# A macaron block on one core: recurrences by channel half, replicated operands copied through DRAM, FFN scales moved from weights to activations

## The chip, the cores and the metric

The kernel runs on one core of one Trainium2 chip. The metric is the device time of one execution in microseconds; the figure quoted is the median of the runs. Engines are named as in the profile: PE is TensorE (matmuls), PEld its weight loads, DVE is VectorE, ACT is ScalarE, POOL is GpSimd, SP is the engine that issues every DMA of this kernel. Each engine runs its own instructions in a fixed order, which the compiler of the kernel language lays down in advance.

## The reference, cut to what matters

The input is 4 sequences of 512 tokens, 128 wide. Six residual stages follow each other; all arithmetic is fp32.

```python
x = x + 0.5 * ffn(layernorm(x))        # 128 -> 512 -> 512 -> 512 -> 128
x = x + mamba(layernorm(x))            # selective state-space layer
x = x + 0.5 * ffn(layernorm(x))        # same weights
x = x + 0.5 * moe(layernorm(x))        # 64 experts, top 8
x = x + attention(layernorm(x))        # 8 heads
x = x + 0.5 * moe(layernorm(x))        # same weights
```

The two parts that the change concerns:

```python
# ffn: a linear layer is (x @ w.T) * s, s one scale per output channel
h = silu(lin(x, w1, s1)) * lin(x, w2, s2)
h = gelu(lin(h, h1, sh1)); h = gelu(lin(h, h2, sh2))
return lin(h, w3, s3)

# mamba: 256 channels d, 16 states n, 512 times t
x_ssm, z = split(x @ in_proj.T)
xc = silu(conv4(x_ssm) + conv_b)
dt_r, B, C = split(xc @ x_proj.T)                       # 1, 16, 16
dt = softplus(dt_r * dt_w + dt_b)
h[t,d,n] = exp(dt[t,d]*A[d,n]) * h[t-1,d,n] + dt[t,d]*B[t,n]*xc[t,d]
y[t,d] = sum_n h[t,d,n]*C[t,n] + xc[t,d]*D[d]
return (y * silu(z)) @ out_proj.T
```

## The kernel before

Everything is held transposed: channels on the 128 partitions, the 512 tokens of one sequence along the free dimension. A sequence is called a batch `b`, 0 to 3. All weights fit in SBUF. A matmul of 128x128 weights with 512 columns appears as two records in the trace[...].

**First half** (`first_half`, L401 on). For each batch: FFN, mamba, FFN again. `ffn` (L219) and `mamba_rest` (L362) are generators; `first_half` interleaves them by hand. While the 16 steps of one batch's recurrence run on DVE and ACT, the `filler` feeds PE with steps of the FFNs of later or earlier batches, as many per step as the table `FILL` says (23 in batch 0, 12 in each of the others). `mamba_first` of the next batch is advanced one generator step at every second recurrence step from step 4 on. `early()` gives instructions a higher priority in the compiler's ordering; the order that comes out is fixed per engine.

**The recurrence.** 256 channels x 16 states = 4096 scans of length 512; one DVE scan instruction does 128 of them. A scan tile holds 32 channels (group `k`, 4 groups in each channel half `c`) by 4 states: partition `32*m + r` is channel `32*k + r` with state `4*m + q`. For this layout the operands must be replicated:

- `rep` (L354, `mamba_spread`): 32 rows of `both` (dt and dt*x, both channel halves, 8 KB a row) are copied from SBUF to SBUF four times, to partitions 0-31, 32-63, 64-95 and 96-127. One DMA per copy, 256 KB each, 16 a batch.
- `B`, `C` (L316-325): written to DRAM (`kept`, L315) and read back in eight DMAs, each with four rows repeated over 32 partitions, 256 KB each.

A step (q, k) then is: two ACT exponentials (`da`, L372, one per channel half), one DVE multiply by B (L374, 128x1024), two DVE scans (L376, 128x512 each), one DVE multiply by C (L377, 128x1024) and two matmuls with the 128x32 matrix `sum4` (L382) that add the four states of a tile into the PSUM accumulators `ys[0]` and `ys[1]`, one for each channel half. After 16 steps PE adds the skip term D*xc (L390), DVE multiplies by silu(z) (L394), PE applies `out_w` (L397) and DVE adds to `xs[b]` (L398). The second channel half is kept with its two 64-row halves exchanged (`HALF`: the split loads of `in_w` and `out_w`, and `skip`), and the copies of `rep` for groups 0 and 1 of the next batch are issued only after step 15.

**FFN scales.** Before the first layernorm the kernel multiplies the scales into the weights (L130-142): a diagonal matrix on DVE, a matmul with ones to spread it over the partitions, a DVE multiply of the weights. From then on activations act on 128x1024 tiles at once: silu (L248), product (L249), gelu (L261).

**PSUM.** `ps_acc` has two rotating banks under one tag, used by the recurrence, the MoE sums and attention; `ps_aux` has two; `pair` has two tiles of two banks.

**Second half** (`second_half`). MoE and attention, PE close to saturated. Its weights are loaded into the SBUF space of the mamba pool once that is free.

Of the kernel before, what the change touches and what calls it, by code (L numbers as in the profile page):

```python
# [29 lines left out]
P = 128  # L30
# [12 lines left out]
HALF = P // 2  # L43
EARLY = 3000
FILL = ((2, 1) * 7 + (1, 1), *[(0, 1, 1, 1) * 4] * 3)
# [11 lines left out]
def macaron(ctx: ExitStack, tc: tile.TileContext, a: dict, out: bass.AP):  # L57
# [7 lines left out]
    ps_acc = ctx.enter_context(tc.tile_pool(name="ps_acc", bufs=2, space=PSUM))  # L65
# [6 lines left out]
    def acc():  # L72
        return ps_acc.tile([P, S], F32, tag="acc", name="acc")
# [14 lines left out]
    nc.sync.dma_start(out=xs[0], in_=a["xT"][:, 0:S])  # L88
    vec = load("vec", [P, NV])
    w1 = load("w1", [P, HID], layer1)  # L90
    w2 = load("w2", [P, HID], layer1)
    h1 = load("h1", [P, NH, HID], layer1)
    h2 = load("h2", [P, NH, HID], layer1)
    w3 = load("w3", [P, NH, D], layer1)

    in_w = layer1.tile([P, 2 * DI], F32, tag="in_w", name="in_w")
    last = 2 * DI - P
    nc.sync.dma_start(out=in_w[:, 0:last], in_=a["in_w"][:, 0:last])
    for i in range(2):
        to, lo = last + i * HALF, last + (1 - i) * HALF  # L100
        nc.sync.dma_start(out=in_w[:, to : to + HALF], in_=a["in_w"][:, lo : lo + HALF])
    xp_w = load("xp_w", [P, NC, 1 + 2 * NST], layer1)
    dt_w = load("dt_w", [1, DI], layer1)
    out_w = layer1.tile([P, NC, D], F32, tag="out_w", name="out_w")
    nc.sync.dma_start(out=out_w[:, 0, :], in_=a["out_w"][:, 0, :])
    for i in range(2):
        to, lo = i * HALF, (1 - i) * HALF
        nc.sync.dma_start(out=out_w[to : to + HALF, 1, :], in_=a["out_w"][lo : lo + HALF, 1, :])
    neg_a = layer1.tile([P, NR, NC, NQ], F32, tag="neg_a", name="neg_a")
    for k in range(NR):  # L110
        for m in range(NM):
            for c in range(NC):
                lo = V_AL + c * NST + m * NQ
                nc.sync.dma_start(
                    out=neg_a[m * R : (m + 1) * R, k, c, :], in_=a["vec"][k * R : (k + 1) * R, lo : lo + NQ]
                )
    for b in range(1, NB):
        nc.sync.dma_start(out=xs[b], in_=a["xT"][:, b * S : (b + 1) * S])
# [9 lines left out]
    ones = layer1.tile([P, P], F32, tag="ones", name="ones")  # L128
    nc.gpsimd.memset(ones, 1.0)
    for w, v, n in ((w1, V_S1, NH), (w2, V_S2, NH), (h1, V_H1, NH), (h2, V_H2, NH), (w3, V_S3, 1)):  # L130
        ps = aux()[:, 0 : n * P]
        for c in range(n):
            d = ln.tile([P, P], F32, tag="diag", name="diag")
            if w is w3:
                nc.vector.tensor_scalar(d, ident, vec[:, v : v + 1], 0.5, ALU.mult, ALU.mult)
            else:
                nc.vector.tensor_scalar_mul(d, ident, vec[:, v + c : v + c + 1])
            nc.tensor.matmul(ps[:, c * P : (c + 1) * P], lhsT=ones, rhs=d, start=True, stop=True)
        if w is w1 or w is w2:
            nc.vector.tensor_mul(w, w, ps)  # L140
        else:
            nc.vector.tensor_mul(w, w, ps.unsqueeze(1).to_broadcast([P, NH, n * P]))
    nc.scalar.activation(neg_a, neg_a, AF.Exp)
    nc.vector.tensor_scalar_mul(neg_a, neg_a, -1.0)

    sum4 = layer1.tile([P, R], F32, tag="sum4", name="sum4")
    nc.vector.tensor_reduce(sum4, ident.rearrange("p (m r) -> p r m", m=NM), AX.X, ALU.add)
    skip = layer1.tile([P, NC, P], F32, tag="skip", name="skip")
    for c in range(NC):
        for i in range(2):  # L150
            to, lo = i * HALF, (i ^ c) * HALF
            nc.vector.tensor_scalar_mul(
                skip[:, c, to : to + HALF], ident[:, lo : lo + HALF], vec[:, V_DD + c : V_DD + c + 1]
            )
# [64 lines left out]
    def ffn(pool, pair, b):  # L219
# [21 lines left out]
        for c in range(NH // 2):  # L241
            p1, p2 = two(), two()
            for ps, w in ((p1, w1), (p2, w2)):
                for i in range(2):
                    product(ps, i, w, xn, c, 1)
            g = pool.tile([P, 2, S], F32, tag="g", name="g", bufs=1)
            with early():
                nc.scalar.activation(g, p1, AF.Silu)  # L248
                nc.vector.tensor_mul(h[:, 2 * c : 2 * c + 2, :], p2, g)  # L249
            yield  # L250
        for w in (h1, h2):
            nxt = pool.tile([P, NH, S], F32, tag="h", name="hn")
            both = [two(), two()]
            for c in range(NH // 2):
# [3 lines left out]
                if c:  # L258
                    with early():
                        for i in range(2):  # L260
                            act = nc.scalar.activation(nxt[:, 2 * i : 2 * i + 2, :], both[i], AF.Gelu)  # L261
                            if not i:
# [6 lines left out]
        with early():  # L269
            nc.vector.tensor_add(xs[b], ps, xs[b])  # L270
        yield

# [3 lines left out]
    def mamba_first(pool, b, made):  # L276
# [15 lines left out]
        with early():  # L292
            for c in range(NC):
                nc.vector.tensor_scalar_mul(cv[:, c, :], xi[:, c, 0:S], col(V_CW + c * DCONV))
                for k in range(1, DCONV):
                    nc.vector.scalar_tensor_tensor(
                        cv[:, c, :], xi[:, c, k : k + S], col(V_CW + c * DCONV + k), cv[:, c, :], ALU.mult, ALU.add
                    )
            for c in range(NC):
# [3 lines left out]
            for c in range(NC):  # L303
                nc.scalar.activation(xc[:, c, :], cv[:, c, :], AF.Silu, bias=col(V_CB + c))
# [8 lines left out]

        kept = dram.tile([2 * NST, S], F32, tag="kept", name="kept")
        nc.sync.dma_start(out=kept, in_=rows[1:])  # L315
        bcs = []  # L316
        for i, name in enumerate(("B", "C")):
            t = pool.tile([P, NQ, S], F32, tag="bcs", name=name, bufs=4)
            for m in range(NM):
                lo = NST * i + NQ * m  # L320
                nc.sync.dma_start(
# [528 lines left out]
```

## Time and profile before

| quantity | value |
|---|---|
| median of 3 runs | 1836.29 us (1835.99 to 1836.46) |
| the profiled execution | 1834.04 us, its span 1832.2 us |
| PE busy | 1717.3 us (94%) |
| DVE busy | 1123.2 us (61%) |
| ACT busy | 785.3 us (43%) |
| POOL busy | 4.3 us |
| DMA moved | 42.27 MB |
| chain that ended last | PE 72%, DVE 17%, ACT 7%, issue 3% |
| recurrence, DVE scans L376 | 128 x 1211 ns = 150.7 us (4.7 us idle before them) |
| recurrence, multiplies L374 and L377 | 64 x 1209 ns and 64 x 1216 ns |
| recurrence, exponentials L372 | 128 x 713 ns |
| gelu L261, silu L248 (128x1024) | 32 x 1021 ns, 16 x 1023 ns |
| table loads on ACT | 1283 ns each |

The span is one execution from its first to its last instruction; 1.8 us of the execution's time lie around it. "Busy" counts an engine's own instructions. PE's busy time is modelled from pipelined matmuls, so a busy PE can still be slower than its best. The chain of waits follows back from the last instruction what each one waited for.

### The profile page before, as it was taken

To read this page: it belongs to the slowest core of one execution; us is meant where nothing else is said; L and a number is where in the kernel's file an instruction comes from. 1 tells how busy PE (TensorE), PEld (TensorE's weight loads), DVE (VectorE), ACT (ScalarE), POOL (GpSimd) and SP (SyncE) were. 2 spreads that over 40 slices of the span, in tenths; PEclk is the share of its full clock that TensorE was granted. 3 is DMA by queue.
4 is the path that set the end of the run, shared out by engine and by line. 5 is a ranking of instruction groups with operands and counts; after the bars stand their busy time and mean duration, and the time that the engine had idled before them with its cause. 6 is when DMAs were issued, how large, how long until landed. Compare 5 with 4: busy or idle time off the path is not lost.

```text
span 1832.2 us, 13288 instructions
## 1 busy us (share of the span) xinstructions
PE 1717.3 (94%) x4466; PEld 749.4 (41%) x4466; DVE 1123.2 (61%) x1976; ACT 785.3 (43%) x1189; POOL 4.3 (0%) x22
## 2 busy tenths in 40 slices
PE   6999899785869999999999999999999999999999
PEld 3333232221224444444455445544554455444443
DVE  3127989798963656556566646665566466565554
ACT  3357647572543223223545345534454444422222
POOL 0000000000000000000000000000000000000000
PEclk9999999997989999999999999999999999999999
DMA  3062224242033000000000000000000000000000
GB/s 96 1 140 48 48 44 93 46 93 46 1 118 112 1 1 0 1 0 1 0 1 1 0 0 1 1 0 0 1 1 6 0 1 1 6 0 1 6 0 6
DMA packets 14441, 42.27 MB, mean 23 GB/s; under 512 B 5068, under 2 KB 6053, under 8 KB 11045
## 3 DMA queue, kind: packets, MB, share of 16 engines
q1 hardware_dynamic: 14373, 41.43, 9.1%
q8 instruction: 35, 0.57, 0.1%
q14 instruction: 33, 0.27, 0.0%
HBM read 23.33 MB, written 1.31 MB: 13 GB/s over the span
## 4 chain that ended last, share of the span: by engine, by line
PE 72%; DVE 17%; ACT 7%; issue 3%; DMA 0%; SPq 0%; DVEq 0%; ACTq 0%
PE acc L559 16%; PE pair L565 16%; PE pair L564 16%; DVE hs L376 7%; PE pair L225 6%; PE aux L620 4%; PE acc L658 4%; DVE hs L374 3%; DVE hs L377 2%; PE aux L648 2%; PE aux L605 2%; PE aux L612 2%; PE aux L196 1%; PE aux L190 1%; PE pair L268 1%
## 5 line engine op out<-in xcount | busy, mean ns | idle before, releaser
L567 ACT ACTIVATE g<-pair 128x512 f32<-128x512 f32 (+1 forms) x368 | 219.6, 597 | 645.6 <-PE pair L565 642.3
L570 DVE TENSOR_TENSOR gr<-g,rw 128x512 f32<-128x512 f32 x352 | 242.7, 691 | 342.0 <-ACT g L567 342.0
L559 PE MATMUL acc<-h,wd 128*128 128x512 f32 x704 | 362.5, 596 | 9.7 <-DVE h L573 9.6
L564 PE MATMUL pair<-xn,wg 128*128 128x512 f32 x704 | 359.9, 593 | 0.0
L565 PE MATMUL pair<-xn,wu 128*128 128x512 f32 x704 | 359.5, 592 | 0.0
L573 DVE TENSOR_TENSOR h<-gr,pair 128x512 f32<-128x512 f32 x352 | 240.4, 686 | 25.3 <-DVE gr L570 0.5
L559 PEld LDWEIGHTS acc<-h,wd 128*128 128x128 f32 x704 | 128.9, 189 | 176.6 <-DVE h L573 112.3
L565 PEld LDWEIGHTS pair<-xn,wu 128*128 128x128 f32 x704 | 133.4, 190 | 161.4 <-issue 158.8
L564 PEld LDWEIGHTS pair<-xn,wg 128*128 128x128 f32 x704 | 126.4, 190 | 120.4 <-issue 117.6
L376 DVE TENSOR_TENSOR_SCAN hs<-da,hs 128x512 f32<-128x512 f32 x128 | 150.7, 1211 | 4.7 <-ACT da L372 4.5
L382 PE MATMUL acc<-hs,sum 128*32 128x512 f32 x256 | 75.6, 672 | 53.3 <-DVE hs L377 52.9
L225 PE MATMUL pair<-h,h 128*128 128x512 f32 x256 | 119.8, 605 | 2.0 <-ACT g L248 1.9
L225 PE MATMUL pair<-hn,h 128*128 128x512 f32 x256 | 116.5, 601 | 4.2 <-ACT hn L261 4.2
L372 ACT ACTIVATE da<-rep,neg_a 128x512 f32<-128x512 f32 x128 | 84.9, 713 | 63.9 <-DVE hs L376 63.7
L620 PE MATMUL aux<-kt,q 128*128 128x512 f32 (+3 forms) x256 | 91.4, 441 | 4.1 <-ACT pt L653 2.7
L633 ACT ACTIVATE p<-p,a_low 128x128 f32<-128x128 f32 (+3 forms) x128 | 70.3, 550 | 31.5 <-DVE a_low L622 31.5
L374 DVE TENSOR_TENSOR hs<-rep,B 128x1024 f32<-128x1024 f32 x64 | 76.8, 1209 | 2.1 <-PE acc L382 2.1
L377 DVE TENSOR_TENSOR hs<-hs,C 128x1024 f32<-128x1024 f32 x64 | 77.8, 1216 | 0.3
L225 PEld LDWEIGHTS pair<-hn,h 128*128 128x128 f32 x256 | 46.7, 190 | 73.6 <-issue 60.9
L225 PEld LDWEIGHTS pair<-h,h 128*128 128x128 f32 x256 | 46.2, 190 | 74.6 <-issue 65.7
L658 PE MATMUL acc<-pt,vo 128*128 128x512 f32 (+3 forms) x256 | 76.2, 433 | 0.0
L225 PE MATMUL pair<-xn,w 128*128 128x512 f32 x128 | 65.1, 646 | 10.9 <-DVE xn L202 7.1
(145 smaller groups left out, 1454.1 us busy)
## 6 DMA issues: line engine op xcount, KB each, us to landing
rep<-both SPq DMA_DIRECT2D x64, 256.0 KB, 5.0
B<-kept SPq DMA_DIRECT2D x16, 256.0 KB, 4.6
C<-kept SPq DMA_DIRECT2D x16, 256.0 KB, 7.6
h<-in_h SPq DMA_DIRECT2D x2, 1024.0 KB, 8.4
wg<-in_wg SPq DMA_DIRECT2D x4, 384.0 KB, 7.3
wu<-in_wu SPq DMA_DIRECT2D x4, 384.0 KB, 7.4
wd<-in_wd SPq DMA_DIRECT2D x4, 384.0 KB, 7.4
wg<-in_wg SPq DMA_DIRECT2D x4, 320.0 KB, 7.2
```

What stands on the lines that cost most here:

```text
L225: m = nc.tensor.matmul(ps[:, i, :], lhsT=w[:, cut] if n == 1 else w[:, k, cut], rhs=h if n == 1 else h[:, k, :], start=k == 0, stop=k == n ...
L374: nc.vector.tensor_mul(h, t[:, 1], bs[:, q].unsqueeze(1).to_broadcast([P, NC, S]))
L376: nc.vector.tensor_tensor_scan(h[:, c, :], da[:, c, :], h[:, c, :], 0.0, ALU.mult, ALU.add)
L377: nc.vector.tensor_mul(h, h, cs[:, q].unsqueeze(1).to_broadcast([P, NC, S]))
L559: nc.tensor.matmul(po, lhsT=w, rhs=h, start=n == 0, stop=n == len(jobs) - 1)
L564: nc.tensor.matmul(pg, lhsT=wg_, rhs=xn, start=True, stop=True)
L565: nc.tensor.matmul(pu, lhsT=wu_, rhs=xn, start=True, stop=True)
L567: nc.scalar.activation(g, pg, AF.Silu)
L570: nc.vector.tensor_mul(gr, g, rw)
L573: nc.vector.tensor_mul(h, g, pu)
L620: nc.tensor.matmul(sc, lhsT=q[:, i * P : n], rhs=kt[:, 0:n], start=True, stop=True)
L658: nc.tensor.matmul(po[:, j * P :], lhsT=vo[:, j, h, :], rhs=pt[:, lo : lo + n], start=h == 0 and j == 0, stop=h == HEADS - 1 and j == NT - ...
```

## The change

**Recurrence.** The loop order becomes channel half `c`, pair of groups, state `q`. A step works on one channel half and two groups (`KP = 2` pairs), so tiles stay 128x1024 for the multiplies and 128x512 for scans and exponentials. Exponentials are asked for in blocks of four (two states, two groups) with high priority. There is one PSUM accumulator `ys`, begun with the skip matmul; the product with silu(z) follows each channel half, in place.

**Copies.** `both` is laid out by channel half and written to a DRAM tile `spread`, one DMA a half. `channels` reads two groups of 32 rows from there, each repeated four times, into a 16 KB-per-partition ring of two tiles. `states` reads one q of B and C at a time into a ring of five tiles. A group's successor is requested at the group's first step, and the next batch's in the last group. `mamba_first` of the next batch advances from step 0. For batch 0 the softplus is cut in two halves.

**FFN.** Weights stay unscaled. silu and gelu take the scale as a per-partition operand and work on 128x512; the product with the second branch becomes a scalar_tensor_tensor with its scale; the output is scaled by `half_s3` in the residual add.

**Loads and set-up.** The exchange of halves goes; `w1` comes before `vec`, `xs[1]` before `h1`; `h1` and `h2` are split in two; `neg_a` takes 8 DMAs instead of 32; what is left of the set-up (`prepare`) is put after four steps of the first FFN. `ps_acc` gets two tags of one bank, `ys` (recurrence, attention) and `po` (MoE).

```diff
-    for w, v, n in ((w1, V_S1, NH), (w2, V_S2, NH), (h1, V_H1, NH), (h2, V_H2, NH), (w3, V_S3, 1)):
-        ps = aux()[:, 0 : n * P]
-        for c in range(n):
-            d = ln.tile([P, P], F32, tag="diag", name="diag")
...
-            nc.tensor.matmul(ps[:, c * P : (c + 1) * P], lhsT=ones, rhs=d, start=True, stop=True)
...
-                nc.scalar.activation(g, p1, AF.Silu)
-                nc.vector.tensor_mul(h[:, 2 * c : 2 * c + 2, :], p2, g)
+                for i in range(2):
+                    f = 2 * c + i
+                    nc.scalar.activation(g[:, i, :], p1[:, i, :], AF.Silu, scale=col(V_S1 + f))
+                    nc.vector.scalar_tensor_tensor(
+                        h[:, f, :], p2[:, i, :], col(V_S2 + f), g[:, i, :], ALU.mult, ALU.mult
+                    )
...
+    def states(pool, b, made, q):
+        kept, _, bcs, _ = made[b][2:]
+        t = pool.tile([P, 2, S], F32, tag="bc", name="bc", bufs=5)
+        by_q = kept.rearrange("(i m q) t -> q m i t", i=2, m=NM)[q]
+        for i in range(2):
+            nc.sync.dma_start(
+                out=t[:, i, :], in_=by_q[:, i].unsqueeze(1).to_broadcast([NM, R, S])
+            )
+        bcs[q] = t
+
+    def channels(pool, b, made, c, pair):
+        _, spread, _, reps = made[b][2:]
+        t = pool.tile([P, 2, 2, S], F32, tag="rep", name="rep", bufs=2)
+        by_k = spread[c].rearrange("(k r) j t -> k r (j t)", k=NR)
+        for i in range(2):
+            nc.sync.dma_start(
+                out=t[:, i].rearrange("p j t -> p (j t)"),
+                in_=by_k[2 * pair + i].unsqueeze(0).to_broadcast([NM, R, 2 * S]),
+            )
+        reps[c, pair] = t
...
                 for step in range(4 * NQ):
+                    group, q = divmod(step, NQ)
+                    if q == 0:
+                        if group < 3:
+                            channels(pool, b, made, *divmod(group + 1, KP))
+                        elif more:
+                            channels(pool, b + 1, made, 0, 0)
+                            states(pool, b + 1, made, 0)
+                    elif group == 3 and more:
+                        states(pool, b + 1, made, q)
                     go(rest)
-                    if step >= 4 and step % 2 == 0:
+                    if step % 2 == 0:
                         go(nxt)
                     filler(FILL[b][step])
```

## The prediction

> **What bounds the kernel now.** I read the page's slices first, then the busy times of each recurrence, then the timeline of the start, then the DMA issues. The slices:
>
> ```profile
> span 1832.2 us, 13288 instructions
> PE   6999899785869999999999999999999999999999
> DVE  3127989798963656556566646665566466565554
> DMA  3062224242033000000000000000000000000000
> ```
>
> From slice 13 on (about 595 us) PE is full and the change touches nothing but bank tags there. All that can move lies before it: a start in which PE is not full, and slices 4 to 11, where DVE is. The busy times in windows cut at the last multiply by C of each batch (columns: window, length, then busy us and count of PE, PEld, DVE, ACT, POOL, granted clock, DMA share, GB/s):
>
> ```profile
> 142.30:241.30 99.00, 90.01 (x223) 30.11 (x221) 90.64 (x87) 60.25 (x73) 0.00 (x0) 0.98 0.31 65
> 241.30:334.00 92.70, 80.05 (x197) 25.95 (x196) 86.03 (x84) 60.71 (x74) 0.11 (x1) 0.98 0.31 65
> 334.00:437.50 103.50, 78.67 (x184) 24.18 (x184) 89.87 (x89) 60.34 (x74) 0.11 (x1) 0.88 0.30 61
> 437.50:525.90 88.40, 67.55 (x165) 21.43 (x166) 78.63 (x73) 39.12 (x48) 0.00 (x0) 0.92 0.03 5
> ```
>
> DVE is idle 8.4, 6.7, 13.6 and 9.8 us in the four batches: little to gain. Batch 0 is held by PE and DVE together. A step of undisturbed recurrence takes 4.5 us. The start and the copies in the timeline (start, us, engine, line):
>
> ```profile
> 0.73 0.38 SPq L88 DMA_DIRECT2D x<-in_xT  x1
> 19.20 2.07 PE L190 MATMUL aux<-x,mean_w 128*128 128x512 f32 x2 [1.95 <-DVE h L142]
> 28.23 7.41 PE L225 MATMUL pair<-xn,w 128*128 128x512 f32 x10 [3.45 <-DVE xn L202]
> 99.44 1.72 SPq L321 DMA_DIRECT2D B<-kept  x4
> 109.95 18.82 SPq L359 DMA_DIRECT2D rep<-both  x16
> 142.32 2.33 DVE L376 TENSOR_TENSOR_SCAN hs<-da,hs 128x512 f32<-128x512 f32 x2
> ```
>
> The first layernorm waits for the scaling of the weights (DVE h L142), not for x. What the DMA engines give, in a stretch of copies to 32 partitions and in one of weight loads to 128 (same columns), and two landing times from the page's issues:
>
> ```profile
> 111.00:128.00 17.00, 15.89 (x38) 6.76 (x37) 0.69 (x1) 5.63 (x6) 0.00 (x0) 1.00 1.00 206
> 540.00:560.00 20.00, 18.41 (x47) 8.13 (x48) 12.42 (x42) 11.31 (x12) 0.31 (x1) 1.00 1.04 393
> ...
> rep<-both SPq DMA_DIRECT2D x64, 256.0 KB, 5.0
> ...
> x<-in_xT SPq DMA_DIRECT2D x4, 256.0 KB, 3.1
> ```
>
> With all 16 engines busy a copy to 32 partitions moves 206/16 = 12.9 GB/s an engine, a load to 128 partitions 393/(16 x 1.04) = 23.6.
>
> [...] The old copies have 32 rows on both sides: 16 engines, and the share of 1.00 agrees. The new `channels` and `states` read with a leading dimension of NM = 4: four engines[...]. No run here shows that yet. [...] the trace has 597 ns for silu without (L567) and 685 to 721 with a bias (L337, L338, L304). I use 690.
>
> **Part 1, the start.** Gone: the 34 diagonal matmul records (10.3 us of PE) and their DVE work. The first layernorm then waits for x, which lands at 0.73 + 3.1 = 3.8 us, and not 19.2. From there to the first FFN matmul it takes the 28.23 - 19.20 = 9.0 us it took: 12.9 against 28.2, so -15.3 us. The matmul needs w1, second in the queue; the silu needs vec, third: both within about 3 us of x. h1 and h2 (2 MB) are wanted some 12 us later, and the old start moved 277 GB/s, so they are in by then. `prepare` is five small DVE operations and a 32-column exponential that lie beside the first FFN's matmuls. 24 fewer DMA issues of `neg_a` (14.96 us for 32 on SP) free that queue, on which nothing waits then. All that follows moves along: `kept` has landed by 99.44 - 15.3 = 84.1 us.
>
> **Part 2, FFN in halves.** ACT: 64 gelus x 690 - 31.0 us = +13, 32 silus x 690 - 16.4 = +5.7, over eight FFNs, 2.4 us each. ACT was busy 61 of 99 us in its fullest batch, which covers it; uncovered it would be 19 us. Against it a layer's first matmul waits for one tile, not two: I give neither a price. DVE: the scalar_tensor_tensor takes 746 ns (L296), so 2 x 746 - 1222 = +0.27 us for each of 16 pairs, +0.5 a batch.
>
> **Part 3, recurrence without its copies.** Per batch still 32 scans of 1.21 us and 32 multiplies of the same, 128 exponentials in all: no DVE work saved. Gone are the skip matmuls in front of the last product (DVE waited 2.9 to 4.0 us for them at the ends) and the wait for `rep` after step 15. Come: two products per batch that wait for the last `sum4` on PE, about 2 us each, and one accumulator bank, so the skip matmul of the next half stands in PE's queue until DVE has done the product; the filler matmuls behind it wait too, but PE has 13 to 25 us free in batches 1 to 3. So each batch is its DVE time + 0.5 + 6 us of waits: 97, 92.5, 96.4 and 85.1 against 99.0, 92.7, 103.5 and 88.4, in all -12.6. After the last step the 2.5 us of skip matmuls are gone: -2.5. The earlier `mamba_first` moves its 16 us of DVE work within the batch only. `po` on one bank: the MoE's first down matmul stands behind four gate and up matmuls of 0.86 us each, which hide the last add of the batch before; nothing, at worst 1 us in each of seven.
>
> **Part 4, the copies.** Four engines[...]. A `channels` request is 64 rows of 4 KB per engine, a `states` request 64 rows of 2 KB. Alone[...] an engine needs 174 and 87 ns a row (23.6 GB/s): 11.1 and 5.6 us a request. [...] In step all the way they get 12.9 GB/s: 318 and 159 ns, 20.3 and 10.2 us. Nothing shows how far they keep step; I take the middle, 15.7 and 7.9, and keep both ends.
>
> Batch 0 begins with four `states` requests, ready at 84.1 before the channels are; `spread` is written (landing 2.4 us: 3.1 less the 0.7 of the bytes, from x) behind them[...]; then `channels` and its landing. First scan: 84.1 + 4 x 7.9 + 2.4 + 15.7 + 2.4 = 136.2, against 142.3: -6.1, so the start's gain is half lost. (Ends: 122.4 and 150.0.) PE's queue still has FFN steps then.
>
> At each of three borders, the last group of a batch asks for one `channels` and four `states`, and the next batch's first group for another `channels`, which stands behind them. In the eight steps, 44 us, of those two groups the four engines owe 2 x 15.7 + 4 x 7.9 + 2.4 = 65.4: 21.4 late. While DVE waits it does the next batch's other work, of which some 6 us are caught up later: +15. (Ends: 47.0, +3; 83.8, +40 with nothing to catch up, for a group then needs 20.3 + 2.4 of its 22 us.) Inside a batch 15.7 + 2.4 fits in 22. ACT's exponentials, high in priority, stand first in its queue while they wait, with gelus behind them and PE behind those; PE's free time covers that. On SP a `channels` request that waits for its buffer would hold back `states`, `kept` and `spread` behind it; the buffer is that of two groups ago, free when it is asked for, so it waits for about nothing (before, L359 waited 62 us for L374 in this place, hidden).
>
> **Sum.** -6.1 - 12.6 - 2.5 + 3 x 15 = +24 us on the profiled execution's 1834.0: 1858. The median before is 2.3 us higher: 1860.
>
> **Rivals.** *The copies keep up* (0.27): the rows run at 174 ns[...]. -19.9 - 12.6 - 2.5 + 9 = -26: 1810. For it: 6.3 MB a batch are then 67 of some 92 us. Against: equal rows, equal order, one start. This is the case on the other side; between it and mine the sign turns at a row about 1.2 times as long as alone. *In step throughout* (0.22): +7.7 - 12.6 - 2.5 + 120 = +113: 1949; the copies alone take 4 x 122 us. *The copy is spread over 16 engines after all* (0.09), so that the change lacks the confinement I read into it: 2.8 and 1.4 us a request, no border wait; PE's own work then holds batch 0 to about 217 us, and -24 - 10 - 2.5 = -37: 1799. *A compiler order that loses the start's gain* (0.04): ACT or PE blocked for 15 to 20 us behind early exponentials: 1836 to 1842.
>
> **How the numbers follow.** Mine has 0.38 with its own range of 1830 to 1900, as the row goes from 1.2 to 1.6 times. Faster by over 0.2% (3.7 us, about what a measurement here tells from no change): 0.27 + 0.09 + 0.03 = 0.39; within it 0.05; slower 0.56. The range, 1797 to 1930, leaves out the upper part of the in-step case.
>
> **What would show it.** First FFN matmul at 13 us; else part 1 is wrong. DMA share about 0.25 with 50 to 100 GB/s while copies run: four engines; a share near 1: sixteen. DVE waiting for `rep` or `bc` by DMA, or for `da`, in the first eight steps of batches 1 to 3 is my case; no such wait refutes it. Landing of a first 512 KB `rep` copy (32 rows and 2.4 us): 8 us alone, 10 in my case, 12.6 in step. The recurrence should end near 549 us, not 526; 500 means that the copies kept up.

## The result, and the profile after

The changed kernel takes 1840.8 us, the kernel before 1834.7 us in runs beside it: the ratio is 1.0032, with a 95% interval of 1.0021 to 1.0042. It is slower by 6 us; 24 were forecast. The profiled execution took 1843.7 us, its span 1841.8.

The page's slices and its chain of waits, after:

```profile
span 1841.8 us, 13185 instructions
PE   8848978787899999999999999999999999999998
DVE  1238889798843655556466656664666466565554
DMA  3021212222041000000000000000000000000000
...
PE 69%; DVE 16%; DMA 7%; ACT 5%; issue 3%; SPq 0%; DVEq 0%; ACTq 0%
```

DMA has come into the chain with 7%; before it had none. In the third slice (92 to 138 us), PE has fallen from 9 tenths to 4. From about 595 us on PE is full again, as forecast. Who waits for the copies is in the answer on waits between 80 and 560 us (engine, line, what it waited for; us, times, longest; lines left out are marked):

```profile
ACT da L367 <- DMA rep<-spread: 92.9, 16, 19.0
...
PE ys L380 <- DVE hs L376: 55.6, 25, 25.5
DVE hs L373 <- DMA rep<-spread: 42.1, 2, 29.0
...
ACT L367 <- DMA rep<-spread: 37.6, 4, 21.9
...
PE pair L251 <- ACT hn L242: 23.6, 6, 11.7
...
DVE x L253 <- PE pair L251: 16.4, 5, 5.7
...
DVE hs L373 <- issue: 9.5, 1, 9.5
...
DVE h L228 <- ACT g L227: 7.9, 3, 4.2
...
DVE h L228 <- PE pair L202: 3.0, 2, 2.8
```

All of these go back to `rep`, by two ways. By the first, ACT stands before exponentials whose `rep` hasn't landed (130.5 us with the table loads that wait in the same place). The gelus (L242) are behind them in ACT's fixed order, PE's next FFN layer (L251) waits for the gelus, and DVE waits for both, with the residual add (L253) and the FFN's product (L228). By the second, DVE waits for `rep` itself (the 9.5 us without a releaser too, as the view of the copies' line, L347, shows), and PE, which has the sums of the recurrence (L380) in its own fixed order, waits for DVE. This is PE's largest wait.

The largest wait is in batch 0. From the timeline, SP's, ACT's and PE's instructions around it (start, us, engine, line; in brackets the idle time before and what ended it):

```profile
84.86 13.47 SPq L336 DMA_DIRECT2D bc<-kept  x8
98.45 3.12 SPq L326 DMA_DIRECT2D spread<-both  x2
110.94 56.02 SPq L347 DMA_DIRECT2D rep<-spread  x8
...
99.28 1.28 ACT L367 ACT_TABLE_LOAD   x1
119.57 0.72 ACT L367 ACTIVATE da<-rep,neg_a 128x512 f32<-128x512 f32 x1 [19.00 <-DMA rep<-spread]
124.64 4.40 ACT L367 ACTIVATE da<-rep,neg_a 128x512 f32<-128x512 f32 x7 [4.36 <-DMA rep<-spread]
129.73 0.72 ACT L367 ACTIVATE da<-rep,neg_a 128x512 f32<-128x512 f32 x1 [0.69 <-DMA rep<-spread]
134.81 4.40 ACT L367 ACTIVATE da<-rep,neg_a 128x512 f32<-128x512 f32 x7 [4.36 <-DMA rep<-spread]
...
98.16 7.99 PE L202 MATMUL pair<-hn,h 128*128 128x512 f32 x18 [0.50 <-ACT hn L242]
131.64 1.92 PE L380 MATMUL ys<-hs,sum 128*32 128x512 f32 x4 [25.48 <-DVE hs L376]
133.49 5.06 PE L202 MATMUL pair<-hn,h 128*128 128x512 f32 x6
138.48 1.05 PE L380 MATMUL ys<-hs,sum 128*32 128x512 f32 x4
```

`spread` is asked for at 98.45 and has landed at 110.94, behind eight requests for states. The two DMAs of the first channels request land at 119.57 and 124.64, those of the next at 129.73 and 134.81: 5.07 us from one DMA to its neighbour. Each is 128 rows of 4 KB; on four engines, as the share below shows, that is 32 rows an engine, 5.07/32 = 158 ns a row. PE does nothing for 25.5 us: it stands before the first sums of the recurrence. Two queues are blocked here. On PE, 18 of the 32 matmul records of an FFN layer (`pair<-hn,h`) have run, and the other 14 stand behind the sums, although the gelus that they read had ended at 99.26; at the 14.00 us that all 32 take elsewhere (run 7) they are about 6 us of work, an estimate. What follows that layer needs gelus, and these stand on ACT behind 17 exponentials; the table load at 99.28 with nothing behind it but waiting is the mark of that blocked queue. In the kernel before, all 32 records and FFN work after them stood ahead of the first sums:

```profile
110.63 14.00 PE L225 MATMUL pair<-hn,h 128*128 128x512 f32 x32 [2.68 <-ACT hn L261]
125.75 3.70 PE L268 MATMUL pair<-hn,w 128*128 128x512 f32 x8 [1.11 <-ACT hn L261]
...
145.97 1.05 PE L382 MATMUL acc<-hs,sum 128*32 128x512 f32 x4
```

How many engines run is in the windows (columns as in the prediction: window, length, busy us and count of PE, PEld, DVE, ACT, POOL, granted clock, DMA share, GB/s), here while nothing but a channels copy goes on:

```profile
114.00:124.00 10.00, 0.00 (x0) 0.00 (x0) 0.00 (x0) 0.72 (x1) 0.00 (x0) 0.50 0.26 97
```

A quarter of 16 engines, at 97/4 = 24 GB/s each. PE and DVE have no instruction in these 10 us.

Where the time went, by three marks: the first scan starts at 127.0 us (before 142.3), the last scan at 521.7 (523.4), and from there to the end of the span it takes 1320.1 us (1308.8). So the scans take 394.7 us from first to last against 381.1, and the remainder has grown by 11.3: in PE's order 132 matmul records of the FFNs come after the last scan, where the kernel before has 88. The three differences add up to the 9.6 us between the two spans; the medians lie 6.1 apart, since the profiled execution was the slowest of the changed kernel's eight.

### The profile page after: what moved, and what is told of

It reads as the page before. It is cut to its first block, busy times and chain, and to the rows that moved or that the text cites. A ratio compares the mean times of both kernels' runs of the same rounds, so it can differ in the third digit from the quotient of the medians.

```text
span 1841.8 us, 13185 instructions
## 1 busy us (share of the span) xinstructions
PE 1713.1 (93%) x4432; PEld 748.3 (41%) x4432; DVE 1114.6 (61%) x1974; ACT 801.1 (43%) x1243; POOL 4.2 (0%) x21
## 4 chain that ended last, share of the span: by engine, by line
PE 69%; DVE 16%; DMA 7%; ACT 5%; issue 3%; SPq 0%; DVEq 0%; ACTq 0%
PE po L561 16%; PE pair L566 15%; PE pair L567 15%; PE pair L202 6%; DVE hs L375 5%; DMA rep<-spread 5%; PE aux L622 4%; PE ys L660 4%; DVE hs L373 3%; DVE hs L376 2%; PE aux L650 2%; PE aux L607 2%; PE aux L614 2%; DMA spread<-both 1%; PE pair L251 1%
## 5 line engine op out<-in xcount | busy, mean ns | idle before, releaser
L561 PE MATMUL po<-h,wd 128*128 128x512 f32 x704 | 362.5, 596 | 10.8 <-DVE h L575 10.7
L561 PEld LDWEIGHTS po<-h,wd 128*128 128x128 f32 x704 | 128.7, 189 | 178.5 <-DVE h L575 114.0
L566 PEld LDWEIGHTS pair<-xn,wg 128*128 128x128 f32 x704 | 126.4, 190 | 120.4 <-issue 117.7
L380 PE MATMUL ys<-hs,sum 128*32 128x512 f32 x256 | 71.2, 642 | 55.6 <-DVE hs L376 55.6
L373 DVE TENSOR_TENSOR hs<-rep,bc 128x1024 f32<-128x1024 f32 x64 | 76.7, 1206 | 52.7 <-DMA rep<-spread 42.1
L376 DVE TENSOR_TENSOR hs<-hs,bc 128x1024 f32<-128x1024 f32 x64 | 77.9, 1217 | 0.1
L242 ACT ACTIVATE hn<-pair,vec 128x512 f32<-128x512 f32 x64 | 38.8, 688 | 87.2 <-PE pair L202 87.1
L660 PE MATMUL ys<-pt,vo 128*128 128x512 f32 (+3 forms) x256 | 76.2, 433 | 0.0
```

The costliest lines, as they stand in the source:

```text
L373: nc.vector.tensor_mul(h, t[:, :, 1, :], bc[:, 0].unsqueeze(1).to_broadcast([P, 2, S]))
L376: nc.vector.tensor_mul(h, h, bc[:, 1].unsqueeze(1).to_broadcast([P, 2, S]))
L561: nc.tensor.matmul(po, lhsT=w, rhs=h, start=n == 0, stop=n == len(jobs) - 1)
L566: nc.tensor.matmul(pg, lhsT=wg_, rhs=xn, start=True, stop=True)
L660: nc.tensor.matmul(po[:, j * P :], lhsT=vo[:, j, h, :], rhs=pt[:, lo : lo + n], start=h == 0 and j == 0, stop=h == HEADS - 1 and j == NT - ...
```

## The experiments

Theory K: the copies' confinement to four engines is the loss. Theory H: the start's gain is real, but exponentials that wait stand before gelus in ACT's order, and PE's idle time is paid later. The two don't exclude each other: K names what is late, H how lateness becomes time. Rival F: the FFN in halves costs what the start gives. Other rivals are named with their runs. All times below are medians; runs of one group have the kernel before beside them (1835.5, 1834.2 and 1834.6 us in the three groups).

| kernel | us | ratio to before, 95% interval | first scan | last scan | from there to the end |
|---|---|---|---|---|---|
| before | 1834.7 | | 142.3 | 523.4 | 1308.8 |
| after | 1840.8 | 1.0032 (1.0021 to 1.0042) | 127.0 | 521.7 | 1320.1 |
| 1 start and FFN alone | 1820.9 | 0.9921 (0.9907 to 0.9934) | 129.3 | 509.9 | 1309.6 |
| 2 recurrence alone | 1851.5 | 1.0086 (1.0073 to 1.0100) | 139.8 | 540.2 | 1310.1 |
| 3 partition 4r+m | 1778.2 | 0.9692 (0.9678 to 0.9705) | 103.0 | 456.4 | 1320.0 |
| 4 ordinary priority | 1843.8 | 1.0043 (1.0030 to 1.0056) | 126.5 | 522.2 | 1314.4 |
| 5 four DMAs a copy | 1795.4 | 0.9789 (0.9775 to 0.9802) | 107.2 | 483.2 | 1309.5 |
| 6 channels on two engines | 1904.6 | 1.0379 (1.0365 to 1.0393) | 135.1 | 596.7 | 1307.1 |
| 7 silus before exponentials | 1826.6 | 0.9956 (0.9944 to 0.9969) | 142.3 | 518.4 | 1306.4 |
| 8 states behind channels | 1844.2 | 1.0042 (1.0028 to 1.0055) | 127.5 | 522.3 | 1320.0 |
| 9 four engines in batch 0 only | 1824.4 | 0.9943 (0.9930 to 0.9957) | 126.3 | 513.1 | 1309.6 |
| 10 four engines in batches 1-3 only | 1810.9 | 0.9872 (0.9858 to 0.9885) | 108.0 | 507.5 | 1304.7 |
| 11 four engines for states only | 1781.7 | 0.9713 (0.9700 to 0.9726) | 117.7 | 474.8 | 1305.1 |
| 12 partition 4r+m, denser filler | 1772.8 | 0.9664 (0.9651 to 0.9677) | 103.4 | 453.4 | 1317.3 |

The three marks are of the profiled execution, in us; it lies within 2 us of the median but for the changed kernel (2.9 above), run 4 (5.1 below) and run 10 (3.1 above).

**1. Start and FFN alone.** The kernel before, with the changed loads, set-up and FFN:

```diff
+    w1 = load("w1", [P, HID], layer1)
     vec = load("vec", [P, NV])
-    w1 = load("w1", [P, HID], layer1)
...
+                    nc.scalar.activation(g[:, i, :], p1[:, i, :], AF.Silu, scale=col(V_S1 + f))
```

> The kernel before with the start and the FFN of the change (scales in activations, order of loads, neg_a in 8 DMAs), its recurrence and SBUF copies unchanged. Theory H (head of the line: the start's gain is real, and the new recurrence spends it because early exponentials that wait for rep stand in ACT's queue in front of gelus, so that PE idles): first FFN matmul at about 14 us as after, first scan at about 128, end about 14 us earlier than before: 1820, at worst 1826. Rival F (halving the activation tiles costs PE and ACT what the start gives): 1832 to 1837, with ACT busy 19 us longer and PE waiting for gelus.

It took 1820.9: the start is worth 14.6 us on its own, and rival F falls. ACT was busy 792.9 us against 785.3 before, and no loss by that shows.

**2. Recurrence alone.** The changed kernel with the weights scaled as before and the old FFN:

```diff
+    vec = load("vec", [P, NV])
     w1 = load("w1", [P, HID], layer1)
-    vec = load("vec", [P, NV])
...
+    for w, v, n in ((w1, V_S1, NH), (w2, V_S2, NH), (h1, V_H1, NH), (h2, V_H2, NH), (w3, V_S3, 1)):
...
```

> The changed kernel with the weight scaling and the FFN of before, so only the recurrence, its copies and the PSUM tags are new. Theory H: the changed kernel's loss without the start's gain: about 6 + 14 = 20 us over before, 1855, with the same hole on PE of some 26 us before the first scan. Rival F: the recurrence is not what costs; 1835 to 1840.

1851.5: the recurrence with its copies costs 16 us. The two parts add up to +1.4 against a measured +6.1; the loss lies in the recurrence.

**3. Sixteen engines by another layout.** Partition `4*r + m` in place of `32*m + r`, so that the 32 rows and not the four repeats lead:

```diff
-                out=neg_a[m * R : (m + 1) * R, :, c, :],
+                out=neg_a[m :: NM, :, c, :],
-        nc.vector.tensor_reduce(sum4, ident.rearrange("p (m r) -> p r m", m=NM), AX.X, ALU.add)
+        nc.vector.tensor_reduce(sum4, ident.rearrange("p (r m) -> p r m", m=NM), AX.X, ALU.add)
-                out=t[:, i, :], in_=by_q[:, i].unsqueeze(1).to_broadcast([NM, R, S])
+                out=t[:, i, :], in_=by_q[:, i].unsqueeze(0).to_broadcast([R, NM, S])
-                in_=by_k[2 * pair + i].unsqueeze(0).to_broadcast([NM, R, 2 * S]),
+                in_=by_k[2 * pair + i].unsqueeze(1).to_broadcast([R, NM, 2 * S]),
```

> The changed kernel with partition 4*r+m for channel r and state m, so that the copies have 32 rows as their outer dimension and go over 16 engines instead of 4; sum4 and neg_a follow; work and order otherwise as they were. Theory K (the confinement to four engines is the cost): share of DMA near 1 while a copy runs, 512 KB landing in 5 us instead of 12.8, waits for rep gone inside the batches and at the borders, and PE's hole before the first scan down from 26 us to under 10: 1805 to 1820. Theory H alone, where only the order counts and not the length of the copies: the hole shrinks only by the shorter copies of batch 0, 1828 to 1835. If neither: 1840.

1778.2, which is 62.6 us below the changed kernel and better than theory K had asked for. The traces show PE, ACT and DVE running their instructions in the same order as in the changed kernel from the first to the last, so this pair differs in its copies alone. A window in which batch 0's channels are copied, and 46 us around the first scan, after this edit and then, last line, as changed:

```profile
98.00:102.00 4.00, 4.00 (x11) 1.81 (x10) 1.31 (x2) 3.89 (x6) 0.00 (x0) 1.00 1.01 404
92.00:138.00 46.00, 39.12 (x100) 13.67 (x98) 40.19 (x40) 33.24 (x45) 0.04 (x1) 1.00 0.28 100
```

```profile
92.00:138.00 46.00, 20.02 (x42) 7.58 (x40) 16.93 (x18) 15.92 (x24) 0.10 (x1) 0.70 0.27 104
```

All 16 engines run, at 404 GB/s; PE's work in those 46 us doubles and DVE's more than doubles. What is left of the waits, between 80 and 480 us:

```profile
PE ys L380 <- DVE hs L376: 32.0, 35, 3.3
...
ACT da L367 <- DMA rep<-spread: 18.1, 7, 6.9
ACT L367 <- DMA rep<-spread: 17.7, 2, 13.7
...
DVE hs L373 <- DMA rep<-spread: 9.0, 2, 5.8
...
PE pair L251 <- ACT hn L242: 5.4, 5, 1.8
```

Each wait shrinks with that for `rep`. DVE's waits in the residual add and the product, 16.4 + 7.9 + 3.0 = 27.3 us as changed, are gone; those for `rep` itself go from 51.6 to 9.0. Before the first sums PE now stands for 2.2 us, with the same 18 records ahead of them:

```profile
97.38 7.99 PE L202 MATMUL pair<-hn,h 128*128 128x512 f32 x18 [0.50 <-ACT hn L242]
107.59 1.05 PE L380 MATMUL ys<-hs,sum 128*32 128x512 f32 x4 [2.22 <-DVE hs L376]
```

The first scan comes 24.0 us sooner, and SP's timeline tells where they lie: `spread` is asked for at 92.45 in place of 98.45 (as changed, SP was still issuing requests for states), it lands in 3.0 us in place of 12.5, and from there to the first scan it takes 7.6 in place of 16.1. Of the 65.3 us by which the last scan comes sooner, 24.0 are the first scan; nearly all of the other 41.3 is DVE's idle time (40.0) in the four batches, as the windows from each batch's first multiply to the next batch's show. As changed:

```profile
124.70:236.80 112.10, 85.79 (x198) 28.13 (x198) 90.07 (x89) 62.58 (x81) 0.10 (x1) 0.87 0.18 66
236.80:335.30 98.50, 80.33 (x194) 26.54 (x194) 87.98 (x87) 64.38 (x85) 0.10 (x1) 0.93 0.18 65
335.30:436.10 100.80, 85.99 (x199) 28.82 (x200) 92.81 (x94) 67.44 (x90) 0.00 (x0) 0.88 0.21 78
436.10:524.20 88.10, 76.68 (x188) 26.16 (x187) 80.11 (x76) 37.65 (x50) 0.00 (x0) 0.94 0.12 42
```

and with sixteen engines:

```profile
100.70:197.60 96.90, 83.05 (x205) 27.57 (x204) 89.90 (x90) 62.50 (x81) 0.10 (x1) 0.96 0.26 83
197.60:292.80 95.20, 83.37 (x211) 27.77 (x210) 94.94 (x96) 72.50 (x94) 0.10 (x1) 1.00 0.25 80
292.80:384.20 91.40, 81.79 (x203) 27.60 (x202) 90.20 (x91) 61.85 (x85) 0.00 (x0) 0.96 0.26 81
384.20:458.90 74.70, 67.03 (x175) 22.66 (x173) 74.64 (x71) 35.17 (x46) 0.00 (x0) 1.00 0.08 28
```

DVE's work is the same, 351 and 350 us; its idle time goes from 399.5 - 351.0 = 48.5 to 358.2 - 349.7 = 8.5 us. The remainder is the same, 1320.0 us for 1320.1, with the same 132 FFN records after the last scan. Runs 5 and 9, whose order leaves 88 as before, have 1309.5 and 1309.6. So the +11.3 there comes from the order that the compiler laid down, not from the waiting.

**4. Exponentials at ordinary priority.**

```diff
-                        with early():
-                            for j in range(2):
+                        for j in range(2):
...
```

> The changed kernel with the exponentials at ordinary priority, everything else the same, the copies still on four engines. Theory H: gelus stand in front of the exponentials again, PE's busy time between 92 and 138 us goes from 20 to over 35 us, and the FFN work left after the recurrence shrinks: 1822 to 1830. Theory K: DVE waits for the same landings (29 us at the start, 13 at a border), so the recurrence ends as late: 1838 to 1845. A third way: exponentials come too late for the scans behind gelus that wait for PE, DVE waits for ACT, and the recurrence ends later: over 1845.

1843.8, no difference from the changed kernel. It decides nothing: in batch 0 the order on ACT came out as it was, 17 exponentials between two gelus, so their priority is not what puts them there, against what I had supposed. (The sums on PE kept theirs, and PE's order stayed too.) Run 7 changes the order itself.

**5. Four DMAs a copy**, the layout of the change kept:

```diff
-            nc.sync.dma_start(
-                out=t[:, i].rearrange("p j t -> p (j t)"),
-                in_=by_k[2 * pair + i].unsqueeze(0).to_broadcast([NM, R, 2 * S]),
-            )
+            for m in range(NM):
+                nc.sync.dma_start(
+                    out=t[m * R : (m + 1) * R, i].rearrange("p j t -> p (j t)"),
+                    in_=by_k[2 * pair + i],
+                )
```

(and the same for `states`)

> The changed kernel, its layout of partitions kept (32*m+r); each copy is asked for as four DMAs of 32 rows, one for each block of 32 partitions, instead of one DMA with a leading dimension of 4. Theory K (the number of engines that a DMA runs on is the whole of the loss): share of DMA near 1 while copies run, at some 206 GB/s as in the kernel before, 2.5 us for the bytes of 512 KB; each request costs SP eight issues instead of two, some 3 us more to landing than in the run with the layout 4*r+m. So 1780 to 1793. Rival P (that run was fast because neighbouring rows go to neighbouring partitions, not for the number of engines): 1815 or more, with copies that take over 8 us.

1795.4, 45.4 below the changed kernel and 2 above the expected range. Rival P falls as the cause of the whole: without any change of layout most of the loss is gone. But the compiler laid down another order here: in batch 0 all of the FFN layer's records and the eight after them stand ahead of the first sums, and 4 exponentials, not 17, between two groups of gelus.

```profile
96.67 14.00 PE L202 MATMUL pair<-hn,h 128*128 128x512 f32 x32 [0.50 <-ACT hn L242]
112.03 3.70 PE L251 MATMUL pair<-hn,w 128*128 128x512 f32 x8 [1.36 <-ACT hn L242]
...
118.26 1.05 PE L383 MATMUL ys<-hs,sum 128*32 128x512 f32 x4
```

So the 45.4 us hold a change of order beside that of the copies; the comparison without it is run 3. The layout of run 3 is another 17 us better. One part of that may be SP, which issues four times as many DMAs, another the rate of DMAs that write 32 partitions each, a third the order. While batch 0's states and channels are copied:

```profile
98.00:102.00 4.00, 4.00 (x11) 1.78 (x10) 0.00 (x0) 0.00 (x0) 0.00 (x0) 1.00 0.91 240
```

240 GB/s on 14.6 busy engines, 16.5 each, against 25 in run 3. Run 11 takes part of the issues away.

**6. Half as many engines for channels.**

```diff
-                in_=by_k[2 * pair + i].unsqueeze(0).to_broadcast([NM, R, 2 * S]),
+            for m in range(0, NM, 2):
...
+                    in_=by_k[2 * pair + i].unsqueeze(0).to_broadcast([2, R, 2 * S]),
```

> The changed kernel with each copy of channels asked for as two DMAs with a leading dimension of 2, so that the dose of the suspected confinement is doubled (states stay on four engines). If the leading dimension sets the number of engines[...]: two engines busy, 256 rows of 4 KB on two engines at 160 ns are 20.5 us a request instead of 10.3. Theory K: 10 us more before the first scan, 10 at each of three borders, 2 to 3 in each of twelve other groups: 1841 + 40 + 30 = 1910, between 1880 and 1950. If the engines are handed out otherwise: no more than 10 us of change.

1904.6, 63.8 above the changed kernel, with two engines running while the first channels are copied:

```profile
112.00:130.00 18.00, 0.00 (x0) 0.00 (x0) 0.00 (x0) 3.23 (x4) 0.00 (x0) 0.50 0.13 49
```

In these three kernels the number of busy engines follows the leading dimension of the source: 32, 4 and 2 give shares of 1.01, 0.26 and 0.13 (16, 4 and 2 engines), and times of 1778, 1841 and 1905. Two DMAs with a leading 2 don't make four engines: a share of 0.13 over 18 us is two engines at a time. The order changed here too (26 records ahead of the first sums), so the 63.8 us are not the engines' alone.

**7. Order on ACT and PE.** Two FFN steps are asked for ahead of the first step, and its four exponentials may not come before their silus. This moves FFN work ahead of the exponentials on ACT and ahead of the first sums on PE:

```diff
-FILL = ((2, 1) * 7 + (1, 1), *[(0, 1, 1, 1) * 4] * 3)
+FILL = ((1, 1) * 2 + (2, 1) * 5 + (1, 1), *[(0, 1, 1, 1) * 4] * 3)
...
+                                    if (b, c, pair, q) == (0, 0, 0, 0):
+                                        after(silus[-1], act)
...
+            filler(2)
             for b in range(NB):
```

> The changed kernel with its work unchanged and its four engines kept, but two FFN steps of the filler are put ahead of the first recurrence step, and the exponentials of that first step may not stand in ACT's order before the silus of those steps. (The run with ordinary priority left ACT's order in this place as it was: 17 exponentials before the next gelu, so it told nothing of the order.) Theory H (order on ACT): PE's busy time between 92 and 138 us goes from 20 to about 40 us, the first scan comes up to 6 us later, and the FFN work left behind the recurrence, 11 us of tail, goes: 1828 to 1834. Theory K alone: the first landing and the borders stay as they are, what PE does meanwhile counts for nothing: 1838 to 1848.

1826.6: 14.2 us gained, with four engines and the same work, a little more than was expected. PE's busy time in the 46 us went from 20.0 to 32.7, not 40: the waits for the first sums and for gelus no longer stand out here, but a new one came, for DVE's residual add (L254), which stands in DVE's order behind the first multiply by B, and that waits for `rep`. PE's timeline:

```profile
96.65 14.00 PE L202 MATMUL pair<-hn,h 128*128 128x512 f32 x32 [0.50 <-ACT hn L243]
112.01 3.70 PE L252 MATMUL pair<-hn,w 128*128 128x512 f32 x8 [1.36 <-ACT hn L243]
115.55 1.88 PE L202 MATMUL pair<-xn,w 128*128 128x512 f32 x4
128.88 2.08 PE L167 MATMUL aux<-x,mean_w 128*128 128x512 f32 x2 [11.45 <-DVE x L254]
```

The first scan moved 15 us later, to 142.3, and the last still came 3.3 us sooner; the remainder is 13.7 shorter, with 100 FFN records after the last scan in place of 132. Theory K alone is refuted here: what PE does while the copy runs counts, and when the first scan starts counts less than its 15 us. How the 14 us divide between ACT's order and PE's the run can't tell, since it changes both.

**8. Order of the requests in batch 0.**

```diff
-            for q in range(2):
-                states(pool, 0, made, q)
+            states(pool, 0, made, 0)
             channels(pool, 0, made, 0, 0)
-            for q in range(2, NQ):
+            for q in range(1, NQ):
                 states(pool, 0, made, q)
```

> The changed kernel, four engines kept, where for batch 0 one request for states is made ahead of the first channels and three behind it (before: two ahead and two behind by the program, all four ahead on SP, because channels wait for spread). Theory O (spread's 12.5 us of landing is the queue behind the states on the same engines): spread lands some 6 us sooner or more, the first scan is at 115 to 120 instead of 127, and the time 6 to 10 us lower: 1831 to 1835. If the order that SP runs is laid down by readiness and not by the program, nothing moves: 1838 to 1844.

1844.2; SP still issued all eight requests for states ahead of `spread`, in the order in which they are ready. So theory O wasn't tested.

**9 and 10. Where the loss lies.** Run 5, with one DMA a copy again in batch 0 alone (run 9, shown for `channels`), or in the others alone (run 10, `b > 0`); `states` likewise:

```diff
+            if b == 0:
+                nc.sync.dma_start(
+                    out=rep, in_=by_k[2 * pair + i].unsqueeze(0).to_broadcast([NM, R, 2 * S])
+                )
+                continue
```

> Copies as four DMAs of 32 rows, as in the run that took 1795, but those of batch 0 as one DMA with a leading dimension of 4 (four engines), as changed. Theory S (the late first landing and the hole that it leaves on PE, filled by nothing later, are the larger part of the 45 us between that run and the changed kernel): first scan at 125 to 128 against 107, PE busy about 20 of the 46 us from 92 to 138, 1820 to 1828. Theory B (borders and later groups are the larger part): 1800 to 1810, PE making up for the hole in later batches.

> The complement: copies of batch 0 as four DMAs of 32 rows, those of batches 1 to 3 on four engines, as changed. Theory S: 1808 to 1818. Theory B: 1828 to 1838. If the two parts add up, this one and its complement lie together 45 us above twice the 1795.

1824.4 and 1810.9: +29.0 for batch 0, +15.5 for the other three, 44.5 together of the 45.4. This is theory S: batch 0 carries the larger part. PE was busy 19.2 of the 46 us in the one and 42.8 in the other. Batch 0 has four of the sixteen channels requests and two thirds of the loss. But run 9 has the changed kernel's order in batch 0 (18 records, then the first sums, 26.33 us idle before them) and run 10 that of run 5, so the 29 us are the longer copies and the order together. Run 7 won 14.2 by order alone.

**11. States alone on four engines** (run 5, with one DMA a copy for `states`):

> Only the states are left on four engines, in all batches, the channels are asked for as four DMAs of 32 rows. If the channels' copies carry the loss, and the states' 8 KB rows of time are hidden by their ring of five: 1790 to 1802 (SP has 24 issues less in each batch). If the states matter because spread stands behind them on their engines, 12 us to landing in batch 0: first scan at about 117, 1803 to 1812.

1781.7, below run 5 and below what was expected. The first scan does come at 117.7, as spread lands behind the states, yet the whole is 13.7 us faster than with all copies on 16 engines by four DMAs. From first to last scan it takes 357.1 us, where run 5 took 376.0. So four engines do the states no harm that counts: with them still confined, 59.1 of run 3's 62.6 us are won, and the channels' confinement carries the loss. Why it is faster than run 5 stays open: SP issues 96 DMAs fewer for the states, but the order differs again (8 exponentials between two groups of gelus).

**12. The filler sooner**, in the kernel of run 3:

```diff
-FILL = ((2, 1) * 7 + (1, 1), *[(0, 1, 1, 1) * 4] * 3)
+FILL = ((2, 1) * 7 + (1, 1), *[(0,) + (1,) * 12 + (0,) * 3] * 3)
```

> The fastest so far (partition 4*r+m, 1778 us) with the filler's twelve steps of batches 1 to 3 at steps 1 to 12, and none in the last three, where before they were at three of every four steps. PE has some 16 us of FFN work left when that run's recurrence ends; asked for sooner, up to 8 us of it (PE's idle time in the last batch) can lie inside: 1770 to 1776. If DVE and ACT are then held up by the denser FFN steps: 1778 to 1784.

1772.8, as expected: 3.4% below the kernel before and 68 us below the changed one. It is 5.4 below run 3, whose own executions lie between 1775.8 and 1782.7.

## Why the prediction was right or wrong

The direction was right, slower, and so was the cause that it rested on: with a leading dimension of 4 the copies ran on four engines (share 0.26 as changed). The size was off by 18 us (+6 for +24), and behind it stand larger errors that partly cancel. At the three marks the forecast was -6.1 us to the first scan, -12.6 + 45 = +32.4 from there to the last and -2.5 after it; the profiled executions show -15.3, +13.6 and +11.3. The steps that failed lie on both sides. Put too high were the row's time, the pile-up at the borders and the waits of the recurrence. Put at nothing were the FFN work that waits behind ACT's and PE's blocked queues, and the FFN work that the compiler's order leaves to the end. That the sign came out right although the copies were faster than forecast owes much to these two, and so is in part luck.

- **Start, -15.3.** Measured: the first FFN matmul at 14.39 in place of 28.23, -13.8; alone worth 14.6. Right. The FFN in halves at no price: right (run 1).
- **Four engines.** Right, as the shares show (0.26 as changed, 1.01 in run 3). The confinement as a whole was forecast at 1860 less 1799, 61 us; run 3 has 62.6. That difference is right by luck, since its terms are not:
- **The row.** This is the term that failed in part 4. I took the middle of 174 and 318 ns for 4 KB, 246, and so 15.7 us a request. The two ends are the rates of 23.6 and 12.9 GB/s an engine from the kernel before; that four engines would slow one another towards the second was an estimate of mine, which no trace showed. Measured 158 ns, 10.1 us a request: faster than my "alone". The first 512 KB DMA was asked for at 110.94 and had landed at 119.57, 8.6 us later, where my own test had 8 for "alone" and 10 for my case. The first scan came at 127.0, not 136.2.
- **What a blocked ACT costs.** "PE's free time covers that" failed, and it is a term that was missing. In the changed kernel DVE waits 27.3 us for FFN work that stands behind ACT's exponentials and PE's sums; in run 3, in the same order, for none of it. The working had nothing of PE's own sums standing ahead of ready FFN matmuls. With the row as measured, it gives the case in which the copies keep up, 1810; the kernel takes 1841. Against that case stand these 27.3 us, the borders (22.6 us against 9) and the remainder (+11.3 against -2.5); the recurrence, which was underrated, takes some of it back. Of the 25.5 us without a matmul in batch 0 run 7 wins back 14 by order alone. The rival with a chance of 0.04, ACT or PE blocked behind early exponentials, named this and its time, 1836 to 1842. That the exponentials' priority is the reason was not confirmed (run 4 didn't move them).
- **The borders.** Three times +15 for requests that pile up on four engines. Measured: 13.1 us at the first, 9.5 at the second, none at the third. Nothing piled up at the first: `spread` was asked for at 216.53 and `rep` at 222.78, and DVE went on at 236.8, so it is one landing after another, bare. The copies of all three batches together cost 15.5 (run 10), not 45. SP's wait for a buffer of `channels`, put at about nothing, comes to 153.1 us in ten waits; no run tells whether it cost time.
- **The recurrence, -12.6.** Underrated. With 16 engines the scans take 353.4 us from first to last, 27.7 less than before. I had added 6 us of waits to each batch's DVE time, 24 in all; DVE idles 8.5. And I had PE hold batch 0 until 217 us; it ended at 198. So "16 engines after all" was put at 1799 and came to 1778.
- **After the recurrence, -2.5.** It became +11.3 between the last scan and the end, since the compiler's order has 44 more FFN records there than before (run 3 has them too, without the hole on PE). The forecast did not ask where that order would leave PE's work.

The recurrence thus ended at 524.2 us (before 525.9), where 549 was expected, and what follows it took longer than expected.

What stays open: how the 29 us of batch 0 divide between the length of the copies, ACT's order and PE's; why the compiler laid down another order from run to run; and how much of run 5's 17 us behind run 3 is the rate into 32 partitions (16.5 GB/s an engine against 25), how much SP and how much the order. That `spread` stands behind the states seems to cost little: in run 11, where it still does, the first scan comes 14.7 us later than in run 3 and the whole takes only 3.5 us more.

## What to carry to other kernels

Read the leading dimension of a DMA's source before its size: here a repeat of four in front, though it saves issues, ran on four engines (share 0.26), and the same bytes with the 32 rows in front (share 1.01) took 62 us off this kernel with every compute engine's order unchanged. When a copy becomes longer, price not only the engine that needs it but everything behind the waiting instructions in each engine's fixed order: here ACT's exponentials held gelus, PE's sums held FFN matmuls that were ready, and giving PE work for its idle 25 us won 14 us although the first scan then came 15 us later. When an edit changes the order that the compiler lays down, its gain is not that of the edit alone; compare the orders in the traces first. A forecast's sum can come near while most of its terms are wrong; hold it against the marks between (first scan, end of the recurrence, remainder), not against the end alone.

## What the runs showed of the hardware that was not expected

- Four engines that copy at once didn't slow one another: 158 ns for a 4 KB row, 4096/158 = 26 GB/s each, as much as two engines in run 6 (49/2 = 24.5) and as in the copy over 16 engines and 128 partitions (404/16 = 25). Sixteen engines on DMAs that write 32 partitions each gave 16.5 each (run 5).
- A DMA over more engines was late behind earlier ones on four of them: as changed, with `spread` asked for at 98.45, the share stayed at 0.26 to 0.27 until 101 us, stood at 1.01 and 1.05 from 102 to 104, and at 0.25 to 0.27 from there to 111. `spread` took 12.5 us from its request to that of the `rep` that waits for it when states on four engines were ahead (98.45 to 110.94; in run 11, where only the states are so confined, 95.83 to 108.31), and 3.0 in run 3 (92.45 to 95.42).
- Issuing was slower too: SP spent 13.47 us on the eight requests for states as changed (13.40 in run 11), and 5.07 us on the same eight in run 3.
- In the stretch without matmuls (106.2 to 131.6 us) the granted clock stands at 1.00 until 110 us and at 0.50 from 111 to 137 us, and the first four matmul records after it (131.64 in the timeline above) take 1.92 us, where the same four at 138.48 take 1.05. Over the span PE was busy 1713.1 us as changed and 1693.5 in run 3, for the same 4432 records in the same order, at a mean granted clock of 0.973 and 0.993: PE's waiting also cost some of its speed.
